# Attention four heads at a time in a three-layer hybrid kernel: float32 scores by row tiles, values by column tiles, row sums by ScalarE

## The chip, the cores and the metric

The kernel runs on one core of one Trainium2 chip. The metric is device time in microseconds (us) of one execution. The engines are TensorE (PE, with its weight loads as PEld), VectorE (DVE), ScalarE (ACT), GpSimd (POOL) and SyncE (SP), which here issues the DMAs. Before the change three runs gave 2176.78, 2178.41 and 2178.43 us; the median is 2178.41.

## The reference

The input x is 2 sequences of 1024 tokens of 512 channels, in float32. Four layers follow, each added to x after a layer norm: a gated linear recurrence, a feed-forward with ternary weights, a differential causal attention, and the same feed-forward again. The change is in the attention alone:

```python
q1, q2 = _split_heads(x @ Wq1, H), _split_heads(x @ Wq2, H)     # H = 16 heads of d = 32
k, v = _split_heads(x @ Wk, H), _split_heads(x @ Wv, H)
q = jnp.concatenate([q1, q2], axis=1)                           # 32 query heads
scores = jnp.einsum('bhqd,bhkd->bhqk', q, jnp.repeat(k, 2, axis=1)) / jnp.sqrt(d)
p = jax.nn.softmax(jnp.where(causal, scores, finfo.min), axis=-1)
y = jnp.einsum('bhqk,bhkd->bhqd', p, jnp.repeat(v, 2, axis=1))
lam = jax.nn.sigmoid(x @ Wlam)                                  # one per token and head
y = y[:, :H] - lam * y[:, H:]
return y.transpose(0, 2, 1, 3).reshape(B, T, D) @ Wo
```

## The kernel before

The program runs the recurrence, the first feed-forward (`feed_forward(0, ...)`), the attention, and the second feed-forward, on tokens in 16 tiles of 128 rows (`xres`). In the attention the work is cut into `pairs` (L666): 2 sequences x 4 groups g x 2 x 2, each of two query heads. For a pair there are these parts.

- `project` (L711) makes queries or keys of 128 channels (four heads) for 512 tokens: 4 float32 matmuls of 512 columns into a bank of the PSUM ring, which ACT rounds to fp32r (`hi`) and DVE subtracts for the rest (`lo`). Eight DMAs write both to DRAM scratch (L738).
- `load_stack` (L742) reads them back as stacks of 128 rows: keys as hi, hi, lo, lo and queries as hi, lo, hi, lo of one head's 32 channels. One fp32r matmul over 128 rows then gives a float32-like product of one head.
- `maxima_step` (L786): scores with queries on the partitions (`s`), the causal mask added on the diagonal (DVE, L804), and the negated maximum of each row (DVE, L808). That is all the scores are used for; each bank is free after the reduction.
- `split_maxima` and `turn_maxima` (L816, L832): POOL splits the negated maxima into three bfloat16 parts, PE turns them so that queries lie along the columns (`mt`), DVE copies them out.
- `weights_step` (L844): for two units, each a block of 128 keys against up to 512 queries, the transposed scores `t` (L858), then three rows of `ones` times `mt` added into the same bank (L865; four of them, in four row groups), then an exponential on ACT (`pr`, L873) and on the diagonal a causal select on POOL (L876).
- `weigh` (L883): the values of a head, with a column of ones for the row sum, are the stationary operand. They are 64 columns wide, and the two heads write partitions 0 to 63 and 64 to 127 of one bank (`y`, L895). After a block's last unit ACT copies y out, and DMAs place each head's 32 rows in `shares` and its sum in `totals` (L915, L920).
- `divide`, `combine` and `project_out` (L925, L937, L953) come once per sequence: reciprocals of the sums (times lambda for the second half of the query heads), a matmul that spreads them over the channels, two products on DVE, the difference on POOL, and the output projection, which DVE adds to `xres`.

All attention matmul results go through one ring of 7 PSUM banks (`b_ring`, L622), except y, which has a bank of its own. PE's order is written out by hand (`manual_schedule`, L1056); the framework orders the other engines. The hand order is

```python
for step in range(STEPS):                 # 6 steps, two units each
    made = weights_step(pair, step)       # t, ones
    for w in waiting:                     # y of the step before
        weigh(*w)
    waiting = made
    for f, args in beside.get((n, step), ()):
        f(*args)                          # projections and the like, by the table at()
    if n + 1 < len(pairs):
        maxima_step(pairs[n + 1], step)   # s of the next pair
```

Ahead of it stands a prologue (first projections, lambdas, values, the first pair's scores) and behind it a tail (the rest of combine and project_out).

Of the kernel before, what the change touches and what calls it, by code (L numbers as in the profile page):

```python
# [42 lines left out]
def kernel(  # L43
# [389 lines left out]
    def normal_stats(b):  # L433
        stats[b] = layernorm_stats(range(b * NQ, (b + 1) * NQ), f"b{b}")
        xts[b] = edge_sb.tile([P, NKC, SEQ], F32, tag="xt", name=f"b_xt{b}")
# [33 lines left out]
    def feed_forward(which, store, first=None, beside=None):  # L469
# [136 lines left out]
        {2: lambda: normal_stats(0)}  # L606
# [7 lines left out]
    HV = HD + 1  # L614
    with ExitStack() as s:


        b_a, b_p, b_b, b_c, b_d = (
            s.enter_context(tc.tile_pool(name=f"b_{i}", bufs=1, reuse_waits="tile")) for i in "apbcd"
# [4 lines left out]
        kd = s.enter_context(tc.tile_pool(name="b_dram", bufs=2, space=bass.MemoryType.DRAM))  # L624

        def ring_bank(name, dtype=F32):
# [3 lines left out]


        causal = b_c.tile([P, P], F32, name="causal")
# [3 lines left out]
            pattern=[[-1, P]], channel_multiplier=1,  # L636
# [5 lines left out]
        head_of = b_c.tile([96 + NH, 2, NKC, P], F32R, name="head_of")  # L642
        nc.gpsimd.memset(head_of.bitcast(F32), 0.0)
        for half in range(2):
            for base in (32 * half, 64 + 32 * half):
                nc.gpsimd.affine_select(
                    out=head_of[:, half], in_=head_of[:, half], compare_op=ALU.not_equal, fill=1.0,
                    base=base, pattern=[[8, 2], [1, 2], [2, 4], [0, HD]], channel_multiplier=-1,
                )
        rows_of = [slice(0, NH), slice(32, 32 + NH)]  # L650


        maxima = []
        for i in range(4):
            m = b_c.tile([P, QB, P], BF, name=f"maxima{i}")
            nc.gpsimd.memset(m, 0.0)
            maxima.append(m)
        w_l = b_c.tile([P, NKC, NH], F32, name="w_l")
        nc.sync.dma_start(out=w_l, in_=wlam.rearrange("(c p) n -> p c n", p=P))

        all_values = b_d.tile([P, NQ * NH * HV + 64 - HV], F32, name="val")
        nc.gpsimd.memset(all_values[:, NQ * NH * HV :], 0.0)
        val = all_values[:, : NQ * NH * HV].rearrange("p (j h d) -> p j h d", h=NH, d=HV)
        nc.gpsimd.memset(val[:, :, :, HD:HV], 1.0)

        pairs = [  # L666
            (b, g, p, par)
            for b in range(NT // SEQ) for g in range(NG) for p in range(2) for par in range(2)
        ]
        scratch, stacks, nmax, lams, totals, shares, factors = {}, {}, {}, {}, {}, {}, {}  # L670

        def load_weights(b, g):
            w = b_b.tile([P, NKC, 3 * P], F32, tag="w_qk", name=f"w_qk{b}_{g}")
            src = wq1 if g < 2 else wq2
            nc.sync.dma_start(
                out=w[:, :, 0 : 2 * P],
                in_=src[:, ts(g % 2, 256)].rearrange("(c p) n -> p c n", p=P),
            )
            nc.sync.dma_start(
                out=w[:, :, 2 * P :], in_=wk[:, ts(g, P)].rearrange("(c p) n -> p c n", p=P)  # L680
            )
            return w

        def values(b, j, w_v):

            xt = xts[b]
            pv = ring_bank(f"pv{b}_{j}")
            for k in range(NKC):
                nc.tensor.matmul(  # L689
                    pv, xt[:, k, ts(j, P)], w_v[:, k, :], start=(k == 0), stop=(k == NKC - 1)  # L690
                )
            nc.vector.tensor_copy(val[:, j, :, 0:HD], pv.rearrange("p (h d) -> p h d", d=HD))

        def load_values(b):
            w_v = b_c.tile([P, NKC, D], F32, tag="w_vo", name=f"w_v{b}")
            nc.sync.dma_start(out=w_v, in_=wv.rearrange("(c p) n -> p c n", p=P))
            return w_v

        def lambdas(b):
            lam = b_c.tile([32 + NH, SEQ], F32, tag="lam", name=f"lam{b}")  # L700
            for e in range(2):
                po = ring_bank(f"pl{b}_{e}")
                for k in range(NKC):
                    nc.tensor.matmul(
                        po[rows_of[1]], w_l[:, k, :], xts[b][:, k, ts(e, BLK)],
                        start=(k == 0), stop=(k == NKC - 1),
                    )
                nc.scalar.activation(lam[rows_of[1], ts(e, BLK)], po[rows_of[1]], AF.Sigmoid)
            lams[b] = lam

        def project(b, g, kind, e, w):  # L711


            n = f"{b}_{g}_{kind}"
            po = ring_bank(f"pq{n}_{e}")
            for k in range(NKC):
                nc.tensor.matmul(  # L717
                    po, w[:, k, ts(kind, P)], xts[b][:, k, ts(e, BLK)],
                    start=(k == 0), stop=(k == NKC - 1),
                )  # L720
            parts = b_p.tile([P, 2, BLK], F32R, tag="parts", name=f"parts{n}_{e}", bufs=2)
            hi, lo = parts[:, 0, :], parts[:, 1, :]
            if kind == 2:
                nc.scalar.copy(hi, po)
                nc.vector.tensor_sub(lo, po, hi.bitcast(F32))
            else:
                scale = 1.0 / math.sqrt(HD)
                nc.scalar.mul(hi, po, scale)
                nc.vector.scalar_tensor_tensor(  # L729
                    lo, po, scale, hi.bitcast(F32), ALU.mult, ALU.subtract  # L730
                )
            if e == 0:

                scratch[b, g, kind] = kd.tile([4, 2, HD, SEQ], F32, tag=f"sc{kind}", name=f"sc{n}")
            sc = scratch[b, g, kind]
            for r in range(2):
                for i in range(4):
                    nc.sync.dma_start(  # L738
                        out=sc[i, r, :, ts(e, BLK)], in_=parts[ts(i, HD), r, :].bitcast(F32)
                    )  # L740

        def load_stack(b, g, kind, i):  # L742


            n = f"{b}_{g}_{kind}_{i}"
            sc = scratch[b, g, kind]
            if kind == 2:
                st = b_a.tile([P, SEQ], F32R, tag="ks", name=f"ks{n}", bufs=4)
                for r in range(4):
                    nc.sync.dma_start(out=st[ts(r, HD)].bitcast(F32), in_=sc[i, r // 2])  # L750
            else:
                st = b_d.tile([P, SEQ], F32R, tag="qs", name=f"qs{n}", bufs=6)
                for r in range(2):
                    nc.sync.dma_start(
                        out=st[ts(r, 2 * HD)].bitcast(F32),
                        in_=sc[i].rearrange("e d n -> (e d) n"),
                    )
            stacks[b, g, kind, i] = st

        def load_stacks(pair):  # L760
            b, g, p, par = pair
            for e in range(2):
                if par == 0:
                    load_stack(b, g, 2, 2 * p + e)
                load_stack(b, g, par, 2 * p + e)

        def operands(pair, e):
            b, g, p, par = pair
            i = 2 * p + e
            return stacks[b, g, 2, i], stacks[b, g, par, i], 4 * g + i  # L770

        def name(pair):
            return "_".join(map(str, pair))
# [3 lines left out]
        max_banks = [  # L777
            [(0, 0, 128, (0, 1)), (1, 0, 256, (0, 1)), (2, 0, 384, (0,)), (2, 0, 384, (1,))],
            [(j, 0, 512, (e,)) for j in (3, 4) for e in range(2)],
            [(4, 512, 128, (0, 1)), (5, 0, 512, (0,)), (5, 0, 512, (1,))],  # L780
            [(5, 512, 256, (0, 1)), (6, 0, 512, (0,)), (6, 0, 512, (1,))],
            [(6, 512, 384, (0,)), (6, 512, 384, (1,)), (7, 0, 512, (0,))],
            [(7, 0, 512, (1,)), (7, 512, 512, (0,)), (7, 512, 512, (1,))],
        ]

        def maxima_step(pair, step):  # L786


            if step == 0:
                nmax[pair] = b_a.tile(  # L790
                    [P, 2, NQ, 2], F32, tag="nmax", name=f"nmax{name(pair)}", bufs=2
                )
            for i, (j, first, nk, heads) in enumerate(max_banks[step]):
                po = ring_bank(f"s{name(pair)}_{step}_{i}")[:, : len(heads) * nk]
                po = po.rearrange("p (e n) -> p e n", n=nk)
                for x, e in enumerate(heads):
# [5 lines left out]
                if first + nk == (j + 1) * P:  # L802
# [7 lines left out]
                    AX.X, ALU.max, negate=True,  # L810
                )

        turned = {}
        n_maxima = [0]

        def split_maxima(pair, half):  # L816
# [326 lines left out]
```

## Time and profile before

| | us |
|---|---|
| median of three runs | 2178.41 |
| the profiled run by itself | 2177.11 |
| its span, first to last instruction | 2175.3 |
| attention, first pq to the second feed-forward's first matmul | 1029.7 |
| of it prologue / loop over the pairs / tail | 67.5 / 929.8 / 32.4 |
| mean granted TensorE clock | 0.995 |

Costliest groups of the attention by the page (count, busy us, mean ns of one):

| group | count | busy | mean |
|---|---|---|---|
| ACT exponential, L873 | 768 | 314.8 | 497 |
| DVE maximum, L808 | 640 | 369.7 | 627 |
| PE y, L895 | 1536 | 291.6 | 501 |
| PE s, L798 | 768 | 206.9 | 391 |
| PE t, L858 | 768 | 198.4 | 357 |
| PE pq, L717 | 384 | 175.8 | 603 |
| POOL select, L876 | 256 | 101.4 | 408 |

In such profiles a busy share counts the time in which an engine had an instruction in flight. PE's instructions overlap: the next starts before the last has drained, so a price is read from start to start in the timeline and not from an instruction's duration. "Idle before, releaser" tells what ended an engine's idle time. The program counts one float32 matmul as two PE instructions, each with its own weight load.

### The profile page before, as it was taken

The page shows a single profiled execution, that of the slowest core. Times are in us where ns is not written, and L with a number is a line of the kernel's source. Part 1 is how long each engine was busy: PE and PEld are TensorE (multiplying, and loading weights), DVE is VectorE, ACT ScalarE, POOL GpSimd, SP SyncE. Part 2 cuts the span into 40 slices and gives each one's busy share as a digit, 9 for nine tenths or more (in the row PEclk, how much of TensorE's full clock was granted, in tenths as well). Part 3 has the DMA queues.
Part 4 walks back from the last instruction along what each step waited for, and adds up shares of the span by engine and source line. Part 5 has one row for each costly group of instructions (what it writes and reads, how often), then busy time and mean ns, then how long its engine had stood idle before and what let it go on. Part 6 is the DMA issues. An engine that isn't in the chain of part 4 may idle for free.

```text
span 2175.3 us, 26073 instructions
## 1 busy us (share of the span) xinstructions
PE 2122.4 (98%) x9072; PEld 1273.5 (59%) x9072; DVE 1126.2 (52%) x2056; ACT 837.3 (38%) x1592; POOL 448.1 (21%) x808
## 2 busy tenths in 40 slices
PE   8999999999999999999999999999999999999998
PEld 3444444688888844555555454454545547888887
DVE  4767676533443235565656574565656763333322
ACT  4344343234334322343444332243434533343433
POOL 0312123122122220111111112121212221222222
PEclk9999999999999999999999999999999999999999
DMA  6111211600000144343434341244443223000000
GB/s 251 58 58 58 88 58 73 246 1 1 1 1 1 35 105 106 98 112 87 121 83 119 76 123 41 73 104 106 104 105 88 64 83 160 0 20 20 1 20 20
DMA packets 77874, 161.41 MB, mean 74 GB/s; under 512 B 19376, under 2 KB 27568, under 8 KB 77744
## 3 DMA queue, kind: packets, MB, share of 16 engines
q1 hardware_dynamic: 77744, 159.75, 25.1%
q8 instruction: 73, 1.20, 0.2%
q14 instruction: 57, 0.47, 0.1%
HBM read 109.08 MB, written 41.94 MB: 69 GB/s over the span
## 4 chain that ended last, share of the span: by engine, by line
PE 86%; DVE 4%; DMA 4%; ACT 2%; SPq 2%; issue 2%; POOL 0%; DVEq 0%; ACTq 0%; POOLq 0%
PE y L895 11%; PE g L511 11%; PE u L511 11%; PE f_out L532 11%; PE t L858 6%; PE s L798 5%; PE ag L260 5%; PE kv L260 5%; PE pq L717 4%; PE pq L260 3%; PE pv L689 3%; PE a_out L408 3%; PE b_out L956 2%; DMA qs<-sc 2%; PE t L865 2%
## 5 line engine op out<-in xcount | busy, mean ns | idle before, releaser
L873 ACT ACTIVATE pr<-t 128x512 f32<-128x512 f32 (+3 forms) x768 | 314.8, 497 | 368.6 <-PE t L865 364.8
L808 DVE TENSOR_REDUCE nmax<-s 128x1 f32<-128x512 f32 (+3 forms) x640 | 369.7, 627 | 54.6 <-PE s L798 54.5
L895 PE MATMUL y<-pr,val 128*64 128x512 f32 (+3 forms) x1536 | 291.6, 501 | 0.8 <-POOL maxima L827 0.8
L526 POOL TENSOR_TENSOR ssq<-ssq,sq 128x512 f32<-128x512 f32 x120 | 155.9, 1299 | 602.5 <-ACT sq L525 602.5
L517 DVE TENSOR_TENSOR h<-h,u 128x512 f32<-128x512 f32 x128 | 88.0, 688 | 362.5 <-PE u L511 356.4
L511 PE MATMUL g<-xs,w 128*128 128x512 f32 x1024 | 261.8, 397 | 0.9 <-ACT xs L461 0.7
L532 PE MATMUL f_out<-w,hs 128*128 128x512 f32 x1024 | 257.7, 394 | 0.3 <-DVE hs L520 0.3
L511 PE MATMUL u<-xs,w 128*128 128x512 f32 x1024 | 257.0, 393 | 0.0
L876 POOL TENSOR_SCALAR_AFFINE_SELECT pr<-pr 128x256 f32<-128x256 f32 x256 | 101.4, 408 | 593.6 <-ACT pr L873 593.3
L858 PE MATMUL t<-qs,ks 128*128 128x512 f32 (+3 forms) x768 | 198.4, 357 | 22.1 <-DVE parts L729 9.6
L511 PEld LDWEIGHTS u<-xs,w 128*128 128x128 f32 x1024 | 192.9, 188 | 43.6
L532 PEld LDWEIGHTS f_out<-w,hs 128*128 128x128 f32 x1024 | 191.6, 188 | 43.9 <-DVE hs L520 1.1
L804 DVE TENSOR_TENSOR s<-s,causal 128x128 f32<-128x128 f32 (+1 forms) x384 | 115.3, 336 | 195.3 <-PE s L798 195.3
L511 PEld LDWEIGHTS g<-xs,w 128*128 128x128 f32 x1024 | 190.5, 188 | 43.9 <-ACT xs L461 0.9
L798 PE MATMUL s<-ks,qs 128*128 128x512 f32 (+3 forms) x768 | 206.9, 391 | 6.2 <-DMA sc<-parts 3.9
L858 PEld LDWEIGHTS t<-qs,ks 128*128 128x128 f32 x768 | 139.2, 188 | 78.2 <-issue 20.8
L717 PE MATMUL pq<-b_xt,w_qk 128*128 128x512 f32 x384 | 175.8, 603 | 0.0
L519 ACT CAST hs<-h 128x512 fp32r<-128x512 f32 x128 | 79.4, 621 | 237.5 <-DVE h L517 237.5
L895 PEld LDWEIGHTS y<-pr,val 128*64 128x64 f32 x1536 | 93.3, 136 | 120.2 <-issue 86.1
L516 ACT ACTIVATE h<-g 128x512 f32<-128x512 f32 x128 | 76.6, 598 | 224.0 <-PE g L511 223.9
L798 PEld LDWEIGHTS s<-ks,qs 128*128 128x128 f32 x768 | 115.0, 190 | 69.4 <-issue 58.6
L520 DVE TENSOR_TENSOR hs<-h,hs 128x512 fp32r<-128x512 f32 x128 | 88.6, 692 | 83.1 <-ACT hs L519 83.1
(151 smaller groups left out, 2145.5 us busy)
## 6 DMA issues: line engine op xcount, KB each, us to landing
qs<-sc SPq DMA_DIRECT2D x128, 256.0 KB, 4.9
w<-w_kept SPq DMA_DIRECT2D x32, 768.0 KB, 8.9
sc<-parts SPq DMA_DIRECT2D x384, 64.0 KB, 1.7
ks<-sc SPq DMA_DIRECT2D x128, 128.0 KB, 4.0
w_kept<-w SPq DMA_DIRECT2D x16, 768.0 KB, 3.2
w<-in_w_gu_dram SPq DMA_DIRECT2D x32, 256.0 KB, 2.8
share<-ys SPq DMA_DIRECT2D x128, 64.0 KB, 2.0
w_in<-in_w_in_t_dram SPq DMA_DIRECT2D x5, 1024.0 KB, 11.0
```

The source lines that it names most:

```text
L260: nc.tensor.matmul(po, w[:, k, ts(c, P)], xt[:, k, :], start=(k == 0), stop=(k == NKC - 1))
L511: nc.tensor.matmul(po, ws[f][:, part, ts(k, P)], xs[:, e, k, :], start=(k == 0 and e == 0), stop=(k == NKC - 1 and e == 1),)
L526: nc.gpsimd.tensor_add(ssq, ssq, sq)
L532: nc.tensor.matmul(po[j], hp[:, e, ts(j, P)], ws[f][:, 2, :], start=(f == 0 and e == 0), stop=(f == NF - 1 and e == 1),)
L717: nc.tensor.matmul(po, w[:, k, ts(kind, P)], xts[b][:, k, ts(e, BLK)], start=(k == 0), stop=(k == NKC - 1),)
L798: nc.tensor.matmul(po[:, x, :], qs[:, ts(j, P)], ks[:, first : first + nk], start=True, stop=True,)
L804: nc.vector.tensor_tensor(diagonal, diagonal, causal.unsqueeze(1).to_broadcast([P, len(heads), P]), ALU.add,)
L808: nc.vector.tensor_reduce(nmax[pair][:, first // BLK, j, heads[0] : heads[-1] + 1], po, AX.X, ALU.max, negate=True,)
L858: nc.tensor.matmul(banks[u, e][:, :nq], ks[:, ts(kb, P)], qs[:, q0 : q0 + nq], start=True, stop=False,)
L873: nc.scalar.activation(pr[:, e, :nq], banks[u, e][:, :nq], AF.Exp)
L876: nc.gpsimd.affine_select(out=pr[:, :, :P], in_=pr[:, :, :P], compare_op=ALU.is_ge, fill=0.0, base=0, pattern=[[0, 2], [1, P]], channel_mu ...
L895: nc.tensor.matmul(y[64 * e : 64 * e + 64, lo:], all_values[:, HV * (NH * kb + h) : HV * (NH * kb + h) + 64], pr[:, e, : BLK - lo], start= ...
```

## The change

The attention is written anew on the same mathematics.

- The unit is a *quad*, four query heads of one group (16 quads, 12 steps each, one block of keys per step). Queries and keys stay in SBUF as float32 (`kq`), four heads in the four quarters of the partitions; DVE alone copies them out of PSUM. The fp32r halves, the DRAM scratch and the stacks are gone.
- Scores `s` and `t` are float32 matmuls over 32 rows, head h in rows 32h to 32h+31, each head into a bank of its own. A step asks the ring of 7 for four banks for t and, in ten of twelve steps, four for s.
- After mask and maximum, each score bank is read once more by ACT: an exponential with the negated maximum as bias, whose output goes to a tile that nobody reads (`unused`) and whose row sum goes to `sums` by `accum_out`. Rows longer than 512 keys have two such parts, which `split` brings to one maximum.
- `split` also makes the reciprocal of the sum (times lambda where it belongs) and splits both numbers into three bfloat16 parts; `turn` transposes them as before; `invert` spreads the reciprocals over the 32 channels of each head by a matmul with `spread`, and ACT copies them out.
- Values are 32 columns wide without the column of ones; four heads write the four quarters of one y bank. DVE multiplies y by the reciprocals straight into `shares`, POOL subtracts the second half. `divide`, `combine` and the copies and DMAs after `weigh` are gone.
- Projections, values and the output projection go in halves of 256 columns; lambdas ride on the values' second half. In a step, beside and scores come before `weigh`. The table of what stands beside is new; the first half of the second sequence's output projection moves into the last quad.

```diff
-        max_banks = [
-            [(0, 0, 128, (0, 1)), (1, 0, 256, (0, 1)), (2, 0, 384, (0,)), (2, 0, 384, (1,))],
...
+        SCORES = [
+            (0, 2, 0, 256),
+            (2, 1, 0, 384),
+            (3, 1, 0, 512),
+            (4, 1, 0, 512),
+            (4, 2, 512, 256),
+            (5, 1, 0, 512),
+            (6, 1, 0, 512),
+            (6, 1, 512, 384),
+            (7, 1, 0, 512),
+            (7, 1, 512, 512),
         ]
+        SCORES_AT = {t: i for i, t in enumerate((0, 1, 2, 3, 4, 5, 6, 8, 9, 10))}
...
+        def scores_step(quad, i):
...
+            for j in range(nj):
+                for h in range(4):
                     nc.tensor.matmul(
+                        banks[h][:, j, :],
+                        queries[j0 // QB][ts(h, HD), ts((j0 + j) % QB, P)],
+                        keys[x][ts(h, HD), :nk],
                         start=True, stop=True,
                     )
+            low, total = (a[quad][:, x, j0 : j0 + nj, :] for a in (nmax, sums))
+            for h, po in enumerate(banks):
+                if nj == 2:
+                    nc.vector.tensor_add(po, po, causal)
+                elif first + nk == (j0 + 1) * P:
+                    nc.vector.tensor_add(po[:, 0, nk - P :], po[:, 0, nk - P :], causal[:, 0, :P])
+                nc.vector.tensor_reduce(low[:, :, h], po, AX.X, ALU.max, negate=True)
+                for j in range(nj):
+                    nc.scalar.activation(
+                        unused[:, :nk], po[:, j, :], AF.Exp,
+                        bias=low[:, j, h : h + 1], accum_out=total[:, j, h : h + 1],
                     )
...
+        def split(quad, half):
...
             if half:
+                nc.vector.tensor_tensor(low, nm[:, 0], nm[:, 1], ALU.min)
+                for x in range(2):
+                    nc.gpsimd.tensor_sub(nm[:, x], low, nm[:, x])
+                nc.scalar.activation(nm, nm, AF.Exp)
+                nc.gpsimd.tensor_mul(total, total, nm)
+                nc.gpsimd.tensor_add(total[:, 0], total[:, 0], total[:, 1])
+            else:
+                nc.gpsimd.tensor_copy(low, nm[:, 0])
+            nc.vector.reciprocal(inv, total[:, 0])
...
+        def invert(quad, half):
...
+            nc.tensor.matmul(
+                r, spread.rearrange("p i d -> p (i d)"), turned[quad, half], start=True, stop=True
+            )
...
+            nc.scalar.copy(inverse[quad, half], r)
...
+        def weights_step(quad, u):
...
+            banks = [ring_bank(f"t{name(quad)}_{u}_{h}") for h in range(4)]
+            for h in range(4):
+                nc.tensor.matmul(
+                    banks[h][:, :nq], keys[ts(h, HD), ts(kb % QB, P)], queries[ts(h, HD), lo:],
+                    start=True, stop=False,
+                )
...
+        def weigh(quad, u, pr):
...
+            for h in range(4):
                 nc.tensor.matmul(
+                    y[ts(h, HD), lo:], vals[b, kb][:, ts(4 * g + h, HD)], pr[:, h, : BLK - lo],
                     start=(kb == 0), stop=last,
                 )
...
+            at(n, (0, 1, 1), [(f, quad, 1) for f in (split, turn, invert)])
+            if n + 1 < len(quads):
+                at(n, (4, 5, 5), [(f, quads[n + 1], 0) for f in (split, turn, invert)])
...
+                made = weights_step(quad, step)
+                for f, args in beside.get((n, step), ()):
+                    f(*args)
+                if n + 1 < len(quads) and step in SCORES_AT:
+                    scores_step(quads[n + 1], SCORES_AT[step])
                 for w in waiting:
                     weigh(*w)
-                waiting = made
+                waiting = [made]
```

## The prediction

> **What bounds the kernel now.** I read the page first: its busy times and the chain that ended last.
>
> ```profile
> PE 2122.4 (98%) x9072; PEld 1273.5 (59%) x9072; DVE 1126.2 (52%) x2056; ACT 837.3 (38%) x1592; POOL 448.1 (21%) x808
> ...
> PE 86%; DVE 4%; DMA 4%; ACT 2%; SPq 2%; issue 2%; POOL 0%; DVEq 0%; ACTq 0%; POOLq 0%
> ```
>
> TensorE (PE) sets the time, and DMA holds 4% of the chain. The change touches attention alone: in the timeline it lies from the first pq matmul (775.20 us) to the second feed-forward's first (1804.9), 1029.7 of the span's 2175.3 us. Busy time by stretch, for its prologue, its loop over 32 pairs and its tail (columns: span, then PE, PEld, DVE, ACT, POOL busy):
>
> ```profile
> 775.20:842.70 67.50, 62.50 (x155) 27.61 (x154) 29.89 (x62) 6.36 (x11) 8.59 (x23) 0.95 0.55 137
> 842.70:1772.50 929.80, 903.88 (x4622) 467.89 (x4620) 552.90 (x1208) 384.20 (x893) 179.05 (x578) 1.00 0.36 91
> 1772.50:1804.90 32.40, 30.73 (x77) 13.96 (x76) 22.35 (x35) 1.87 (x2) 10.39 (x9) 1.00 0.34 126
> ```
>
> In the loop PE is busy 97%, ACT 41%, DVE 59%: the other engines wait for PE, and a bank of the ring is nearly always free when PE wants it (PE's waits before t sum to some 20 us). Then the PE timeline of one step:
>
> ```profile
> 972.56 1.43 PE L858 MATMUL t<-qs,ks 128*128 128x512 f32 x4
> 973.92 0.40 PE L865 MATMUL t<-mt_s,ones 3*128 3x512 bf16 x4
> 974.25 1.94 PE L895 MATMUL y<-pr,val 128*64 128x512 f32 x8
> 976.12 0.40 PE L836 MATMUL mt<-ident,maxima 128*128 128x128 bf16 x4
> 976.33 0.94 PE L798 MATMUL s<-ks,qs 128*128 128x256 f32 x4
> 977.10 0.97 PE L858 MATMUL t<-qs,ks 128*128 128x512 f32 x4
> 978.01 0.39 PE L865 MATMUL t<-mt_s,ones 3*128 3x512 bf16 x4
> 978.33 1.94 PE L895 MATMUL y<-pr,val 128*64 128x512 f32 x8
> ```
>
> Prices per 512 columns: the four `ones` matmuls, in four row groups, take 0.40 us together, so they run at once. A float32 matmul is two instructions of 0.43 us (pq: eight in 3.43 us, start to start), so one costs 0.86. The eight y instructions are two units of two heads: 1.94 us is four slots of 0.43, so the two column tiles run side by side. An fp32r product (t, s) is one instruction of 0.23. The step from 974.25 to 978.33 is 4.08 us against 3.63 of such prices: 0.45 us goes into changes of tile shape. ACT and DVE:
>
> ```profile
> L873 ACT ACTIVATE pr<-t 128x512 f32<-128x512 f32 x384 | 201.7, 601 | 276.8 <-PE t L865 276.8
> ...
> L349 ACT ACTIVATE a<-ag,two 128x512 f32<-128x512 f32 x16 | 11.0, 685 | 47.3 <-PE ag L260 47.3
> ```
> ```profile
> L808 DVE TENSOR_REDUCE nmax<-s 128x1 f32<-128x512 f32 x384 | 249.7, 680 | 54.5 <-PE s L798 54.5
> ```
>
> Back to back they start every 0.48 us (ACT) and 0.60 us (DVE) at 512 columns: about 0.05 + 0.00083 N and 0.065 + N/960. A bias from a tile (`two`, L349) costs 0.09 more.
>
> **PE's work.** Before: the loop's work beside the pairs is 42 projections x 3.43 = 144, values 27.4, lambdas 7, out-projection 27.4, combine 4, transposes 9: 219 us. So a pair costs (929.8 - 219)/32 = 22.2, four heads 44.4.
> After, per four heads, if four row tiles and four column tiles run at once: t 4608 columns at 0.86/512 = 7.7; s 4864 columns (two rows padded) 8.2; y 7.7 (it was 15.5: this is the saving); `ones` 1.9; transposes and the new spread matmul 0.9; 12 steps of 0.5 for shape changes (the float32 t is new after y) 6: 32.4. Sixteen times, less 8 for the last, which computes no following scores: 510. Beside it lie the same 144 of projections, values with lambdas 28.3, batch 0's out-projection 27.4, half of batch 1's 13.7, transposes 9: 222. **PE alone: 732 instead of 930, 198 less.** DVE's reductions, masks and copies come to some 38 us per four heads, about as now; POOL has fewer and longer selects. Neither decides.
>
> [...]
>
> **ACT's work.** The sums add 48 ACTIVATEs per four heads: 19456 columns x 0.00083 + 48 x (0.05 + x). x is 0.09 for the bias from a tile plus what writing a sum costs; no row shows that. It lies between 0 and a small ACTIVATE by itself (128x4 at L117, 0.30); I take 0.11, nearer the bias's 0.09, so x = 0.2: 28.2 us. With the exponentials of the weights (17.8) and copies 1.5 this is 47.5 us per four heads, 732 in all: as much as PE has. It would just fit if nothing waited.
>
> **The wait that is added.** The ring keeps seven banks. A step now takes four for t and four for s, where s was freed by one DVE reduction and now is held through mask, reduction and an ACTIVATE. PE's order is t, ones, beside, s, y, t: when the next t comes, four s banks are held, three are free, and **the fourth head's t waits for the first s bank**. From the end of the s stream, by start times of the trace: 0.27 until DVE starts (ACT's first exponential starts 0.26 after `ones` has streamed), mask (0.21 or 0.6), reduction 0.60, 0.15, ACTIVATE 0.60 + x, 0.05 (PE followed ACT's 0.60 so at 846.52). At 512 columns without a mask that is 1.67 + x; y and its changes cover 1.06 when y is 512 wide and 0.4 when it is 128. Over the ten score steps the waits are 1.9, 0.6, 1.0, 1.0, 1.9, 0.6, 0.6, 0.6, 0.6, 1.0 = 9.8, plus 12 x (two steps hold two ACTIVATEs each): 12.2 us per four heads, fifteen times: **184**. `ones`, s and y queue behind the waiting t on PE, and everyone waits for them.
> The fourth s waits likewise for t's first exponential (0.26 + 0.60 + 0.05 = 0.9, less 0.1) where no projection stands between, 5 steps of 12: 60, less the steps with values or transposes: 45. turn and invert now stand together, so PE waits for the DVE copy between them: 0.25 + 0.34 + 0.15, twice per four heads: 24. The chain before the second turn (last scores of step 10, DVE, ACT, a rescaling on POOL and ACT, a reciprocal, the split: some 12 small operations of 0.2 us each, L825's row, behind 3.3 us of reductions and sums) takes about 7 us; PE's own steps 11, 0 and 1 take 7.9, so I cost it at nothing; late by 1 us it would cost 15. In ACT's queue the exponentials of the next t stand behind the score ACTIVATEs, or the other way: 0 to 75, I take 40. Together 293.
>
> **What goes at the ends.** The 384 scratch writes and 256 stack reads lie beside PE in the loop: nothing there; SP's queue, where the weight loads stay, only empties. In the prologue PE waits for them some 5 us (804 to 808); with lambdas in the values it becomes 6.9 + 8.2 + 24 x 1.75 + 5 = 62, so 5.5 less. The tail loses divide, combine and half the out-projection: 16 instead of 32.4.
>
> **Sum.** Loop 732 + 293 = 1025, 95 more; ends -22: +73 on the profiled run's 2177.1 (span 2175.3), which lies 1.3 under the median of 2178.41: **2250 us.** The bounds of the unknowns: without the sum's price (x = 0.09) 20 us less, at 0.30 (x = 0.39) 35 more; ACT's order -40 or +35; shape changes 0.35 to 0.6 per step, -29 to +19. So 2180 to 2330.
>
> **Rivals.** (1) *The banks come free in time*, and PE's saving shows. For it: ACT is idle 59%, DVE 41%. Against: the s bank's path has three more latencies and the ring no more banks. It decides at 220 us of waits (198 + 22); less the other 109 that is 111 for the t waits, 0.74 us in each of 150 score steps against my 1.2: below it the kernel is faster. With half of my waits 2105, with none but invert's 1981. (2) *ACT becomes the bound*: writing a sum costs 0.30 or more, or the score ACTIVATEs of two-row banks hold up DVE's next reduction: 60 to 100 us more, 2310 to 2350. (3) *Float32 tiles don't run four at a time* (the trace shows two columns of float32 and four rows of bf16): t and s at pairs cost 16 x 15.9, 2500; y alone at pairs 2370. (4) *It does what it says but what it removes was hidden*: the DRAM stacks are; this is in the sum.
>
> **How the numbers follow.** Forecast 0.57 (2180 to 2300), rival 2 0.13, rival 3 0.05, rival 1 0.25. The range takes the forecast, rival 2 and the upper half of rival 1: 2085 to 2345. Within 0.2% (what this measurement can tell from no change) 0.03, out of the low edge of the forecast and the high edge of rival 1; slower 0.73, faster 0.24.
>
> **What would show it.** Right: PE's idle before t names ACT and DVE of the score path, 100 us and more; PE under 85% busy in the loop, ACT near 70%; y at 0.86 us for four heads. Wrong: PE still 95% busy (rival 1); ACT over 85% with score ACTIVATEs over 0.9 us (rival 2); s or t of four heads over 1.1 us without waiting (rival 3).

## The result and the profile after

The changed kernel takes 2386.45 us (median of 4 runs, 2382.98 to 2400.24) against 2178.42 for the kernel before (4 runs, 2176.78 to 2180.27): a ratio of 1.097, interval 1.092 to 1.101. The forecast was 2250, with 2085 to 2345 as range. The direction was right, the size was not.

The profiled run's span is 2384.6 us, 209.3 more than before. First the engines, the granted TensorE clock by slices, and the chain that ended last, from the page after:

```profile
PE 2261.2 (95%) x11078; PEld 1317.1 (55%) x11088; DVE 1184.3 (50%) x2120; ACT 1297.0 (54%) x3063; POOL 405.6 (17%) x573
...
PEclk9999999999999988999898989998789879999999
...
PE 16%; DVE 0%; ACT 0%; DVEq 0%; issue 0%
```

The clock is no longer full in the middle slices, which are the attention. The chain can be followed back over 16% of the span only, so it says nothing of the attention here. The three stretches, with the columns of the table in the prediction (span; PE, PEld, DVE, ACT, POOL busy; granted clock; DMA share; GB/s):

```profile
775.10:847.60 72.50, 66.03 (x323) 48.20 (x323) 50.44 (x115) 35.34 (x101) 1.77 (x8) 0.95 0.13 38
847.60:2000.10 1152.50, 1057.28 (x6481) 492.94 (x6479) 607.54 (x1242) 815.05 (x2276) 150.45 (x360) 0.88 0.03 8
2000.10:2014.60 14.50, 14.03 (x69) 12.05 (x65) 5.49 (x12) 0.00 (x0) 1.27 (x1) 1.00 0.73 299
```

The loop grew by 222.7 us, prologue and tail together shrank by 12.9: that is the 209. PE looks 92% busy, yet the run with PE alone, below, puts its work there at some 800 us. A matmul that waits inside a pipelined group, or runs at half clock, counts as busy here: six instructions of t stand for 2.62 us, a projection for 3.48 instead of 1.99 (next section). The clock of 0.88 is the sign that was missing from the forecast. ACT is busy 71%, as forecast. What PE waited for, by the waits of the PE queue (us in total, times, longest):

```profile
PE t L860 <- ACT unused L784: 67.5, 45, 3.5
PE r L838 <- DVE mt_s L832: 17.6, 28, 1.0
...
PE pq L699 <- DMA w_qk<-in_wk_dram: 6.1, 1, 6.1
```

The costliest groups (busy us, mean ns of one, idle before and its releaser):

```profile
L784 ACT ACTIVATE unused<-s,nmax 128x512 bf16<-128x512 f32 (+2 forms) x768 | 462.4, 602 | 259.4 <-DVE nmax L782 238.9
L782 DVE TENSOR_REDUCE nmax<-s 128x1 f32<-128x512 f32 (+2 forms) x640 | 398.6, 659 | 76.5 <-PE s L769 70.0
L860 PE MATMUL t<-kq,kq 32*128 32x512 f32 (+3 forms) x1536 | 302.6, 581 | 68.9 <-ACT unused L784 67.5
...
L784 ACT ACTIVATION_READ_ACCUMULATOR unused<-s,nmax 128x1 f32 x768 | 152.5, 199 | 0.0
```

A sum costs ACT an instruction of its own (199 ns). One step of the timeline shows the rest (start, us, operation):

```profile
1207.95 2.48 DVE L782 TENSOR_REDUCE nmax<-s 128x1 f32<-128x512 f32 x4 [0.63 <-PE s L769]
...
1208.74 0.69 ACT L784 ACTIVATE unused<-s,nmax 128x512 bf16<-128x512 f32 x1 [1.02 <-DVE nmax L782]
1209.06 0.31 PEld L860 LDWEIGHTS t<-kq,kq 32*128 32x128 f32 x6 [0.84 <-issue]
1209.06 0.99 PE L860 MATMUL t<-kq,kq 32*128 32x256 f32 x7
1209.32 0.19 ACT L784 ACTIVATION_READ_ACCUMULATOR unused<-s,nmax 128x1 f32 x1
1209.55 0.69 ACT L784 ACTIVATE unused<-s,nmax 128x512 bf16<-128x512 f32 x1
...
1209.59 0.28 PE L866 MATMUL t<-mt_s,ones 3*128 3x256 bf16 x3
...
1209.89 0.37 PE L860 MATMUL t<-kq,kq 32*128 32x256 f32 x1
...
1210.10 0.27 PE L866 MATMUL t<-mt_s,ones 3*128 3x256 bf16 x1
...
1211.17 0.69 ACT L784 ACTIVATE unused<-s,nmax 128x512 bf16<-128x512 f32 x1
...
1211.85 1.20 ACT L872 ACTIVATE pr<-t 128x256 f32<-128x256 f32 x4
```

The score sums start 0.81 us apart (1208.74, 1209.55), x = 0.33 in the prediction's terms and not 0.2. The last head's t stands apart from the others, as forecast. And t's exponentials (L872) come only after all four sums, at 1211.85, though three heads' t was complete some 2 us earlier, with their `ones` at 1209.59. Four row tiles in float32 do run at once: in such timelines the eight instructions of t at 512 columns take 0.96 us from start to next start, those of y 0.99, those of s 1.07, where eight of pq over the whole array took 3.43 before.

### The profile page after: what moved, and what is told of

The parts are those of the page before. It is cut to its first block, busy times and chain, and to the rows that moved or that the text cites. A ratio compares the mean times of both kernels' runs of the same rounds, so it can differ in the third digit from the quotient of the medians.

```text
span 2384.6 us, 29868 instructions
## 1 busy us (share of the span) xinstructions
PE 2261.2 (95%) x11078; PEld 1317.1 (55%) x11088; DVE 1184.3 (50%) x2120; ACT 1297.0 (54%) x3063; POOL 405.6 (17%) x573
## 5 line engine op out<-in xcount | busy, mean ns | idle before, releaser
L784 ACT ACTIVATE unused<-s,nmax 128x512 bf16<-128x512 f32 (+2 forms) x768 | 462.4, 602 | 259.4 <-DVE nmax L782 238.9
L782 DVE TENSOR_REDUCE nmax<-s 128x1 f32<-128x512 f32 (+2 forms) x640 | 398.6, 659 | 76.5 <-PE s L769 70.0
L860 PE MATMUL t<-kq,kq 32*128 32x512 f32 (+3 forms) x1536 | 302.6, 581 | 68.9 <-ACT unused L784 67.5
L872 ACT ACTIVATE pr<-t 128x512 f32<-128x512 f32 (+3 forms) x768 | 322.1, 497 | 68.7 <-PE t L866 67.1
L769 PE MATMUL s<-kq,kq 32*128 32x512 f32 (+2 forms) x1536 | 271.5, 593 | 2.0 <-ACT unused L784 1.2
L860 PEld LDWEIGHTS t<-kq,kq 32*128 32x128 f32 x1536 | 107.2, 202 | 268.0 <-ACT unused L784 174.0
L699 PE MATMUL pq<-b_xt,w_qk 128*128 128x256 f32 x768 | 227.0, 448 | 9.0 <-DMA w_qk<-in_wk_dram 6.1
L699 PEld LDWEIGHTS pq<-b_xt,w_qk 128*128 128x128 f32 x768 | 162.5, 222 | 88.6 <-ACT unused L784 41.8
L892 PE MATMUL y<-pr,val 128*32 128x512 f32 (+3 forms) x1536 | 184.3, 555 | 0.0
L769 PEld LDWEIGHTS s<-kq,kq 32*128 32x128 f32 x1536 | 115.2, 199 | 86.5 <-ACT unused L784 33.5
L784 ACT ACTIVATION_READ_ACCUMULATOR unused<-s,nmax 128x1 f32 x768 | 152.5, 199 | 0.0
```

The costliest lines, as they stand in the source:

```text
L699: nc.tensor.matmul(po, w[:, k, :], xts[gi // NG][:, k, e * BLK + x * HALF :][:, :HALF], start=(k == 0), stop=(k == NKC - 1),)
L769: nc.tensor.matmul(banks[h][:, j, :], queries[j0 // QB][ts(h, HD), ts((j0 + j) % QB, P)], keys[x][ts(h, HD), :nk], start=True, stop=True,)
L782: nc.vector.tensor_reduce(low[:, :, h], po, AX.X, ALU.max, negate=True)
L784: nc.scalar.activation(unused[:, :nk], po[:, j, :], AF.Exp, bias=low[:, j, h : h + 1], accum_out=total[:, j, h : h + 1],)
L860: nc.tensor.matmul(banks[h][:, :nq], keys[ts(h, HD), ts(kb % QB, P)], queries[ts(h, HD), lo:], start=True, stop=False,)
L872: nc.scalar.activation(pr[:, h, :nq], banks[h][:, :nq], AF.Exp)
```

## The clock

The half-speed stretches (granted clock 0.50) are whole multiples of one window of 3.41 us in this trace: 84 windows or 286.7 us of the loop, against one or 3.4 in the loop before. Four windows in a row, along the boundaries at which the clock changes:

```profile
1212.72:1216.14 3.42, 2.76 (x32) 1.03 (x30) 2.77 (x8) 1.60 (x5) 0.64 (x1) 1.00 0.00 0
1216.14:1219.55 3.41, 3.41 (x20) 1.26 (x16) 1.39 (x4) 2.62 (x11) 0.91 (x3) 1.00 0.00 0
1219.55:1222.97 3.42, 3.42 (x10) 2.50 (x8) 0.25 (x1) 2.07 (x4) 2.46 (x9) 0.50 0.00 0
1222.97:1226.38 3.41, 2.72 (x32) 1.21 (x31) 2.23 (x5) 0.00 (x0) 0.00 (x0) 1.00 0.00 0
```

And PE in them:

```profile
1216.01 0.64 PE L892 MATMUL y<-pr,val 128*32 128x256 f32 x8
1216.58 2.62 PE L860 MATMUL t<-kq,kq 32*128 32x512 f32 x6
...
1219.93 3.48 PE L699 MATMUL pq<-b_xt,w_qk 128*128 128x256 f32 x8
```

In the window from 1216.14 PE is "busy" throughout, but t's six instructions stand there 2.62 us, where eight take 0.96 when they don't wait. In the next window a projection takes 3.48 us instead of 1.99. I priced every matmul of the loop by its size (0.43 us for a float32 instruction of 512 columns over the whole array, a quarter for one of four tiles, half of either for bfloat16, which before started 128 columns every 0.056 us against 0.109 in float32) and summed by window. Of the 44 windows at full speed before a half-speed one, 41 streamed under 42% of the time; of the 211 before another full-speed one, 10 did. In eleven of the runs below the split is about as sharp (26 of 33 against 3 of 260 in the kernel before with sums). So in these loops half clock comes one window behind PE's waiting. PE was hardly ever idle for a whole window: for 3.5 us once in this loop, and otherwise for 2.6 us at the longest.

Its price: steps with the same matmuls, some of them partly at half speed, fit 0.39 (standard error 0.03) us more per us at half speed, so 287 us cost about 110. Cutting the steps in other ways gives 0.36 to 0.43, or 100 to 125 us; in most other runs the slope was 0.35 to 0.52, but 0.7 to 0.9 in the four runs below whose queues were out of order. This is an estimate from a fit: a step that waits longer also draws more half clock, and no run changes the clock alone. The granted 0.50 alone, if PE streamed throughout, would make it 143 (half of 286.7), an estimate too.

## The experiments

My theory at this point: PE waits for score banks, which are held through mask, maximum and sum, and half clock follows the waits. Rivals: the four-head form itself costs PE more than was priced; or ACT and DVE set the pace by their own queues, whoever holds the bank. Each time in the table but the first two is that of one run; the changed kernel's four runs spread over 17 us, so smaller differences are not read. The loop is taken from the first t to the end of the last y.

| run | time | loop | of it at half clock |
|---|---|---|---|
| before | 2178.4 | 929.3 | 3.4 |
| after | 2386.5 | 1150.4 | 286.7 |
| no sums | 2221.0 | 987.2 | 126.3 |
| sums without read | 2361.0 | 1124.1 | 262.8 |
| beside last | 2405.0 | 1168.7 | 324.3 |
| before, with sums | 2401.4 | 1153.8 | 157.0 |
| fill | 2412.8 | 1178.7 | 146.8 |
| turn apart | 2401.3 | 1165.5 | 317.4 |
| no sums, turn apart | 2219.1 | 984.5 | 150.2 |
| PE alone | 2039.2 | 805.6 | 3.4 |
| sums off the bank | 2324.4 | 1090.2 | 215.0 |
| ring of six | 2552.0 | 1313.2 | 457.4 |
| maxima freed, in order | 2177.7 | 944.0 | 88.7 |
| both freed, in order | 2358.0 | 1125.6 | 300.4 |

### What the sums cost

No sums:

```diff
-                for j in range(nj):
-                    nc.scalar.activation(unused[:, :nk], po[:, j, :], AF.Exp, ..., accum_out=...)
+                nc.gpsimd.memset(sums[quad], 1.0)      # at i == 0
```


> The changed kernel without the score ACTIVATEs; the row sums are set to 1 by a memset, so the division by the softmax sum is left out. Theory (the score bank is held through ACT's sum, PE waits for it before t, and the waiting lowers the granted clock): the waits before t go, the clock in the loop rises from 0.88 to 0.97 or more, the loop falls from 1152 to about 800, the whole to 2010 to 2080. Rival (the four-head float32 form is slow or lowers the clock by itself): above 2300, clock still near 0.9.

Sums without the read (`accum_out` dropped, sums set to 1):

> The changed kernel with the score ACTIVATEs but without accum_out, so 768 reads of the accumulator (152 us of ACT) go; the row sums are set to 1, so the division by them is left out. Theory: the bank is held 0.34 us less per ACTIVATE, so the waits shrink by a third and the clock with them: 2270 to 2330. Rival (ACT's busy time is the bound): all of the 152 us come off, 2230.

The sums in the kernel before (with three buffers for the split maxima instead of four, for room; the sums go nowhere):

```diff
+                for x, e in enumerate(heads):
+                    nc.scalar.activation(
+                        unused[:, :nk], po[:, x, :], AF.Exp, bias=nmax[pair][...],
+                        accum_out=sums[pair][...],
+                    )
```


> The kernel before with the same 768 score ACTIVATEs with accum_out added after each maximum (768 of up to 512 columns; the sums are not used, all else as before; one of four buffers of the split maxima is given up for room). Theory: banks of this ring too are held through ACT, and PE waits: 2280 to 2400 and the clock under 0.95. Rival (only the four-head form suffers): under 2220.

Measured 2221.0, 2361.0 and 2401.4. The sums cost 165 us; of this the separate reads are 25, less than expected. In the old kernel, with heads in pairs and PE otherwise unchanged, the same instructions cost 224. So the form with four heads is not what makes the kernel slow. But without sums the changed kernel is still 43 above before, where I had expected it some 100 to 170 below: something else eats PE's saving.

### PE alone

Masks and maxima go too; nobody reads the score banks. This run builds on "no sums, turn apart", further below, which its text calls the run above.

```diff
-                nc.vector.tensor_add(...)              # masks
-                nc.vector.tensor_reduce(low[:, :, h], po, AX.X, ALU.max, negate=True)
+                nc.gpsimd.memset(nmax[quad], -80.0)    # at i == 0
```


> The kernel of the run above without masks and maxima on the scores too (the maxima are set to a constant, 80, the sums to 1; both are left out of the computation). The score banks are written by PE and read by nobody, so PE waits for the exponentials of t alone. Theory (PE alone needs 732 us in the loop, as forecast, and the rest of the added time is waits for held banks and the half clock behind them): the loop takes 740 to 790, the whole 1970 to 2040, clock above 0.99. Rival (the four-head form costs PE more than was priced, or draws the half clock by itself): the loop 850 or more, the whole above 2090.

2039.2: at the edge of the theory's time, with a loop of 805.6 above its 740 to 790. Its stretch:

```profile
847.40:1653.00 805.60, 802.99 (x6477) 389.23 (x6476) 113.71 (x273) 347.32 (x833) 147.66 (x370) 1.00 0.04 11
```

PE saves 124 us, not 198, and the clock stays full with all float32 tiles running: the half clock doesn't come from the tiles. By tile, start to next start: pq 158.7 (priced 144), out-projection 45.0 (41), values 31.2 (28); the halves of 256 columns cost more than whole ones, by more shape changes as I read it, which I had not counted. Each step's t with `ones`, s and y take the rest; of that some 20 to 40 us are s standing behind t's exponentials (512 columns take some 1.8 us right after `ones` and 1.07 after a projection; all s right after `ones` lose 19 us by this, all s 40).

### The clock, by filling

```diff
+            for _ in range(4):
+                nc.tensor.matmul(banks[0], ones, filler, start=True, stop=True)   # ahead of t
```


> The changed kernel with four more bf16 matmuls of 128x512 (ones times a constant tile) into the first bank of t ahead of its float32 matmuls, in each of the 192 steps; the real t starts the bank anew, so the result is the same. They are 192 x 4 x 0.22 = 169 us of PE work, put where PE has just finished y and often waits for the fourth bank of t. Theory (the clock is halved in stretches because PE waits so often; the changed kernel lost some 140 us to it): the granted clock of the loop rises from 0.88 to 0.96 or more and the time falls in spite of the added work, to 2250 to 2360. Rival (the halving follows from something else, such as the float32 tiles in all four quarters at once): the clock stays at 0.90 or under, and the added work shows: 2430 to 2560.

Half-speed time fell from 287 to 147 us and the clock of the loop rose from 0.88 to 0.94, but the added 169 us showed in part: 2412.8, 26 slower. Here the clock did follow PE's activity, but buying it with empty matmuls cost more than it gave. The theory's numbers and the rival's, time and clock, were both missed: by name PE still waits 31.7 us at t, instead of 67.5.

### Order and turn

> The changed kernel with PE's order t, ones, s, y, beside in place of t, ones, beside, s, y: the projections stand between the scores and the next t and cover its wait in the steps that have one, while s comes sooner after t and waits more for t's exponentials. Theory: 2330 to 2370. Rival (the four-head form by itself): within 0.5% of 2386.

The edit moves the `beside` loop behind `weigh`. 2405.0, no gain. By name PE's waits at t fall from 67.5 to 6.6 us and s waits 11.4 for t's exponentials; the rest hides in pipelined groups and in 324 us at half clock. The sum of the named waits is no measure of what waiting costs.

Turn and invert a step apart (steps 1 and 2, 5 and 6), on the changed kernel and on that without sums:

```diff
-            at(n, (0, 1, 1), [(f, quad, 1) for f in (split, turn, invert)])
+            at(n, (0, 1, 2), [(f, quad, 1) for f in (split, turn, invert)])
-                at(n, (4, 5, 5), [(f, quads[n + 1], 0) for f in (split, turn, invert)])
+                at(n, (4, 5, 6), [(f, quads[n + 1], 0) for f in (split, turn, invert)])
```


> The changed kernel with invert one step after turn (steps 2 and 6 instead of 1 and 5), so that PE no longer stands at the spread matmul until DVE has copied the turned sums. Theory (this wait is on the path, 17.6 us of it in 28 places, as forecast with 24): 2350 to 2375. Rival (the step's other waits take its place): within 5 us of 2386.

> The kernel without the score exponentials (sums set to 1, so the division by the softmax's sums is left out), 2221.0 us, with invert one step after turn. There PE stood 49.6 us at the spread matmul, up to 3.4 us at a time. Theory (those waits are on the path, and the clock falls behind them): 2130 to 2180, with a granted clock above 0.98. Rival (the four-head form itself is no faster than the pairs): 2205 to 2225.

2401.3 and 2219.1: no gain in either. The second is the lesson. Without sums PE's longest wait had been this one:

```profile
PE r L834 <- DVE mt_s L828: 49.6, 32, 3.4
PE t L856 <- DVE nmax L783: 23.6, 30, 1.0
```

With turn and invert apart it is gone, and the time is 2 us less; PE waits at other places:

```profile
PE t L856 <- DVE nmax L783: 24.0, 31, 1.0
PE s L770 <- DVE nmax L783: 13.7, 21, 1.0
```

Half-speed time did not fall either, so the clock above 0.98 that was expected did not come. A wait that ended with work in DVE's queue only moved when it was taken away at one place: DVE has the same work as before.

### Banks or queues

One bank less (`bufs=6`), and, in a second run, the sums on a constant tile instead of the bank:

> The changed kernel with six banks in the ring instead of seven; nothing else differs. Theory (PE waits because t and s together want one bank more than the ring has): now the third head's t waits for the first score bank too, with some 0.25 to 0.5 us less of cover in each of 150 score steps, and the third s for the first exponential, with the half clock behind both: 2430 to 2520. Rival (ScalarE or VectorE by their own time set the pace, banks don't matter): 2380 to 2400.

```diff
-                        unused[:, :nk], po[:, j, :], AF.Exp,
+                        unused[:, :nk], still[:, :nk], AF.Exp,
```


> The changed kernel with the same 768 exponentials with a sum on ScalarE, each still behind its maximum (its bias), but reading a constant tile in SBUF (bfloat16) instead of the score bank, so that a bank is free after mask and maximum; the sums are set to 1 afterwards, so the division by the softmax's sums is left out. Theory (the sums cost what they do because they hold the score banks): close to the kernel without sums at all, which took 2221: 2215 to 2270. Rival (ScalarE's own time and queue: 0.81 us for one at 512 columns, and the exponentials of t behind them): 2340 to 2400.

Ring of six: 2552.0, 166 slower. Banks matter. Sums off the bank: 2324.4, so of the 165 us only 62 vanish with the holding; 103 remain, with ACT's load still in its queue (a sum's exponential took 633 ns on average off the bank, 602 on it, so the 103 are a little high). Next, VectorE's part likewise on a constant tile, and the sums put back on PE alone:

> The kernel without sums and with invert apart from turn (2219; sums set to 1), with as many mask and maximum instructions of the same sizes on VectorE, but on a constant tile in SBUF, so that nobody reads the score banks. The causal mask, the maxima and the sums are left out of the computation. Between this kernel and the one without the VectorE work at all (2039) lie 180 us. Theory (masks and maxima cost because they hold banks, and the half clock comes behind the waits): 2035 to 2085, clock above 0.99. Rival (VectorE's own time: the copies of projections and turned sums stand behind the reductions): 2130 to 2220.

> The kernel without masks, maxima and sums (2039) with the 768 exponentials with a sum put back on ScalarE, on a constant bfloat16 tile, behind no score: ScalarE has its full load and holds no score bank. The same parts are left out of the computation. Theory (ScalarE by itself needs more than PE: at 0.81 us for 512 columns the sums take 34.4 us per four heads, with 17.8 for the exponentials of t and 1.5 for copies 54, sixteen times 859, against PE's 806 in this loop): the loop 870 to 950, the whole 2105 to 2185. Rival (ScalarE's load hides behind PE once it holds no banks): the loop 806 to 830, the whole 2040 to 2065.

2320.1, 101 above the kernel with the same work on the banks, and 2379.2, 340 above PE alone. Both tests were spoilt: with nothing of PE's to wait for, these instructions ran ahead in their queues (by the traces a step's reductions start 204 us before its scores, its sums 216, as medians; in the changed kernel 1.5 and 2.3 us after them), and what PE needs stood behind them. The waits of the first show it; in the second, s waits 119.8 us for t's exponentials:

```profile
PE t L858 <- DVE kq L708: 41.3, 13, 5.6
PE t L858 <- DVE kq L706: 36.0, 12, 5.8
```

To free the banks and keep work in its place, VectorE first takes four numbers from each bank:

```diff
+                nc.vector.tensor_copy(tiny[:, ts(h, 4)], po[:, 0, :4])    # for the four banks
...
-                nc.vector.tensor_reduce(low[:, :, h], po, AX.X, ALU.max, negate=True)
+                nc.vector.tensor_reduce(low[:, :, h], view, AX.X, ALU.max, negate=True)
```


> The changed kernel in which VectorE first takes four numbers out of each of the four score banks (four small copies, after which the banks are free) and then makes masks and maxima of the same number and sizes on a constant tile; ScalarE makes its 768 exponentials with a sum on another constant tile, behind these maxima as before. So both engines have their full load in the old place of the queue, and no score bank is held for it. Masks, maxima and sums are left out of the computation. Theory (the banks are what PE waits for; the engines' own time costs what the sums off the bank cost, 103): 2039 + 103 = 2140, 2120 to 2200. Rival (the queues of VectorE and ScalarE set the pace, whoever holds the bank; sums off the bank took 2324): 2270 to 2330.

> The same without the exponentials with a sum, and with invert a step after turn: VectorE frees the score banks with small copies and then has the load of masks and maxima on a constant tile, behind them in its queue. Masks, maxima and sums are left out of the computation. To be set against 2219 (masks and maxima on the banks) and 2039 (none). Theory (the 180 us between these are banks held): 2040 to 2090. Rival (they are VectorE's queue: copies of projections stand behind reductions, and pq's bank is held in their place): 2170 to 2230.

2412.9 and 2310.3: still out of order, as in this stretch of VectorE in the second, where nine reductions surround the one copy that PE's t waits 3.93 us for:

```profile
1206.55 3.65 DVE L788 TENSOR_REDUCE nmax<-causal 128x2 f32<-128x512 f32 x6
1210.12 0.41 DVE L706 COPY kq<-pq 128x256 f32<-128x256 f32 x1
1210.45 1.86 DVE L788 TENSOR_REDUCE nmax<-causal 128x1 f32<-128x512 f32 x3
```

So the small copies were made to write into the very tile that the reductions read (`causal[:, 0, ts(h, 4)]` in place of `tiny`), which fixes the order:

> As the run before without sums (masks and maxima on a constant tile, score banks freed by small copies; masks, maxima and sums left out of the computation), but the small copies write into the constant tile that masks and maxima read, so the work of a step on VectorE can't move ahead of its scores nor the copies ahead of the maxima before them. There 2310, because reductions had moved ahead and PE stood 55 us at copies of projections. Theory (the 180 us that masks and maxima cost are banks held): 2040 to 2090. Rival (they are VectorE's time in its queue): 2170 to 2230, the time with the maxima on the banks being 2219.

> The same with the 768 exponentials with a sum on ScalarE, on a constant tile, each behind its maximum, and invert in the step of turn: both engines fully loaded in order, no score bank held beyond the small copies (masks, maxima and sums left out of the computation). Theory (banks held make the difference to the changed kernel's 2386, save the 103 of ScalarE's own time): 2120 to 2200. Rival (the engines' queues set the pace): 2270 to 2330, as with the sums off the bank, 2324.

Without sums 2177.7; with them 2358.0. A step's reductions now start 2.4 us after its scores. The same instructions in another order took 2310.3 and 2412.9: order alone is worth 133 and 55 us. Against the banks held in order (2219.1 and 2386.5), freeing them gains 41 and 28 us. So neither number of the theory came; the rival is nearer. But the small copies load VectorE with some 98 us of busy time that the kernels with held banks don't have (700 against 602 us in the loop without sums, 705 against 608 with them), so 41 and 28 rather understate what the holding cost. For ACT's sums, then, the larger part of the loss is the queue and not the held score bank (103 of 165); for masks and maxima, how the 180 us between 2039.2 and 2219.1 divide is not shown. Both stretches:

```profile
847.60:1791.50 943.90, 898.23 (x6476) 427.89 (x6475) 699.85 (x1837) 346.73 (x836) 159.92 (x402) 0.95 0.03 10
```
```profile
846.00:1971.50 1125.50, 974.82 (x6476) 440.79 (x6475) 704.83 (x1838) 825.29 (x2276) 161.39 (x418) 0.87 0.03 8
```

ACT goes from 347 to 825 us busy and the loop grows by 182, although nobody's score bank waits for ACT. Not all of the 182 is ACT: with sums, invert stands beside turn again, where without them it stands apart. In the second PE waits where the queues feed it:

```profile
PE r L846 <- DVE mt_s L840: 96.5, 32, 5.3
PE s L771 <- ACT pr L880: 49.6, 32, 3.2
```

The first is 17.6 us in the changed kernel and 0.7 without sums and with invert apart; both in order with invert apart was not run. The second is a wait for a bank after all, one of t's: its exponential stands behind sums in ACT's queue.

No version here computes the whole and beats either kernel: masks and maxima, 180 us, use up PE's 124 before a sum is made.

## Why the prediction was wrong

The loop was forecast as 732 + 293 = 1025 and took 1152.5. Two steps of the sum failed in size: PE's own work, and the clock, which was put at nothing. The cause named for the largest wait is borne out only in part, and that the waits came out nearly at the size forecast is luck in part. That the waits would outweigh the saving, and the kernel be slower, was right.

- **"PE alone: 732 instead of 930" was too low.** It is 805.6, or some 765 to 785 without the waits for t's exponentials, which the prediction had among its waits (45 forecast, 20 to 40 in that run). The halves of projections, priced like whole ones, are 20 us of the difference.
- **The clock was no term at all.** The sum took every matmul at full speed. About 110 us by the estimate above (0.39 x 287) is the largest missing piece. The trace of before had the loop at 1.00; only its prologue, at 0.95, held a stretch of half clock (6.83 us from 806.80, where PE had stood idle for 3.87 up to 808.81). Beside the forecast's own 293 us of waits that row should have raised the question.
- **The waits were about the right size under the wrong names.** 1150 less 806 less 110 leaves 235, and with the 20 to 40 above some 255 to 275 against 293; this is as good as the 110 is. But the step "the fourth head's t waits for the first s bank: 184" is not borne out at that size. The row is there (67.5 us by name), and one bank less costs 166; yet freeing the score banks gave only 28 in order, small copies included, or 62 for ACT's hold. "ACT's order, 40" and "neither decides" (of DVE and POOL) failed in turn: DVE's maxima in order, off the banks, cost 139 us over PE alone (small copies and half clock included), ACT's sums 103 to 180 (the latter with invert beside turn in the one run and apart in the other).
- **x was mis-sized**: 0.33, not 0.2. With it ACT needs 19456 x 0.00083 + 48 x 0.38 + 17.8 + 1.5 = 53.7 us per four heads, and 825 in all, counted as in the forecast with no sums for the last: a little more than PE's 806. (The text of the run with the sums alone says 859, which counts the last; ACT was busy 815 us in the changed loop.) Rival 2 (ACT the bound, 2310 to 2350) was nearest in time and half right: its signs, ACT over 85% and ACTIVATEs over 0.9, did not come (71%, 0.69 plus the read), but ACT's queue holds back what PE needs.
- **Right**: four float32 tiles at once (rival 3 refuted, 0.96 to 1.07 us), the tail (14.5 against 16), the added waits naming the score path (though 67.5 us of them and not 100 and more). That the removed DRAM stacks are worth nothing in the loop, no run tests by itself. PE's starts do not keep to the kernel's order in these rows: `ones` of three heads start at 1209.59, ahead of the fourth head's last t at 1209.89, though the kernel writes all of t ahead of `ones`. The prologue is 72.5 instead of 62, of which 6.1 is PE waiting for the first key weights' DMA. "PE under 85% busy" was a bad sign to choose: busy time hid both waits and half clock.

What stays open: the split between banks and queues, since each run that frees a bank also changes what the queues meet (by 98 us of copies on VectorE, and for ACT by the place of invert); and the price of the half clock, which is a fit. That a planned order (t's exponentials ahead of the sums in ACT's queue) would help was not tried.

## What to carry to other kernels

When PE's work shrinks, add up each other engine's instructions in its queue, its extra ones too, before the waits: with ACT at 825 against PE's 806 the saving could hardly show, and counting banks explains only part. Price PE's waits twice where they come densely: once as time, once as the half clock behind them (here 235 us left for the waits, and some 110 by the fit for the half clock). Ask of a wait that is to be taken away whether the queue behind it gets shorter: here two such edits gained nothing.

## What the runs showed of the hardware

- Half clock (0.50 granted) came in windows of 3.41 us. In the changed kernel's loop 41 of the 44 full-speed windows ahead of a half-speed one streamed under 42% of the time, by prices from the traces, against 10 of the 211 ahead of another full-speed one; PE was idle for as long as a window only once there (3.5 us). Filling its waits with matmuls took the half-speed time from 287 to 147 us.
- An exponential with `accum_out` was two instructions here; the read took 199 ns on average, and sums of 512 columns started 0.81 us apart.
- Four float32 row tiles or column tiles of 512 columns took 0.96 to 1.07 us together, and instructions of three row tiles started ahead of one of the fourth that stands before them in the kernel's order (1209.59 against 1209.89).
- The framework's order of the other engines shows as much as the chip: reductions that depended on nothing of PE's stood some 200 us ahead in their queue and delayed what PE needed, 2310.3 against 2177.7 us for the same work in order.
